# Two tiles' values weighed together in a Perceiver block's main loop, with a third place for the weights

## The chip, the cores and the metric

The kernel runs on one core of one Trainium2 chip. The metric is the device time of one execution in microseconds (us); the kernel before took 1071.89 us as the median of three runs (1071.27 to 1072.69). A core has five engines that run side by side, each with its own instruction stream: TensorE (PE in the profile; its weight loads are listed apart as PEld), VectorE (DVE), ScalarE (ACT), GpSimd (POOL) and SyncE (SP), which here only issues DMAs.

## The reference

One Perceiver layer on 128 queries of width 512: a cross attention to a context of 12544 rows, a self attention of the 128 queries, and a mixture of experts. The change lies in the cross attention alone (16 heads of width 32; the first 257 context rows are an image part with weights of their own, the other 12287 are the text part):

```python
q = rms_norm(linear(x, q_w, q_b), norm_q_w).reshape(B, L, NH, HD)
k = rms_norm(linear(ctx_txt, k_w, k_b), norm_k_w).reshape(B, -1, NH, HD)
v = linear(ctx_txt, v_w, v_b).reshape(B, -1, NH, HD)
...
img_x = attention(q, k_img, v_img)
txt_x = attention(q, k, v)
out = (txt_x + img_x).reshape(B, L, DIM)
return linear(out, o_w, o_b)
```

`attention` takes softmax of q·k / sqrt(32) over the context rows and weighs v with it. Each key row is divided by the root of its mean square, so the kernel needs a sum of squares for each context row. Everything is in fp32.

## The kernel before, in words

**Blocks and tiles.** The context comes transposed, in 25 blocks: block 0 is the image part (three tiles), blocks 1 to 24 are the text part, 512 rows each (511 in the last), in four tiles of 128 rows. The text tiles are numbered from t = 3; block 5 begins with tile 19, block 24 (`LAST`) with tile 95. In a block, j (0 to 3) is the tile's place. The main loop (line 1535) runs over the tiles of blocks 2 to 23. While it scores and weighs block b, it makes keys and values of block b + 1.

**Keys and values: seven products.** Instead of eight quarter products a block's keys (and likewise its values) come from seven, in the manner of Strassen and Winograd. `weight_sums` prepares sums of the weights once; `ctx_sums` (line 1058) prepares four sums of the context's quarters for each block on GpSimd: s1 and s2 for products 5 and 6, s4 and s3 for products 3 and 7. All four lie in one tile, `xsum`, with one buffer, so the sums for the next block wait until the last product of this one that reads them. `product` (line 1072) is one group of four matmuls in the program (eight in the trace, line 1082) and writes a PSUM bank from `bank()`, a ring of three that the sums of squares use too. Some products go on in the bank of an earlier one: 2 in that of 1, 3 in that of 5, 4 in that of 7. `step` (line 1131) issues product k for keys, values or both, and what empties the bank: ScalarE copies 1 and 2 (lines 1139, 1110, 1101), VectorE does the rest (1144, 1147, 1112, 1103). Once a half of the keys is complete (steps 3 and 4 for keys), ScalarE squares it (`squares`, line 1121), and `add_squares` (line 1123) adds the four chunks of 128 channels in two instructions on GpSimd.

**Norms.** `key_norms` (line 1010) lets TensorE add the squares over the channels, for two tiles at a time ([0, 1] or [2, 3]), VectorE scales the sums (line 1029), and GpSimd raises them to the power −1/2 into `rinv` (line 818).

**A tile.** `scores` (line 1159) is 16 matmuls on strips of 32 rows of the array into `ps_x`, the only score buffer (four PSUM banks). `weights` (line 1246) has VectorE multiply by `rinv`, subtract a per-query bound `m_bc` and write `p` (line 1255), and ScalarE take the exponential in place (line 1263). `weigh` (line 1266) is 16 matmuls on strips of 32 columns that add v weighted by p into one PSUM bank. `into_sums` (line 1424) adds p into the sum of weights on GpSimd (line 1433). The tiles `p` have two buffers in the pool `two`.

**The order.** Every instruction of the loop is kept in program order on its engine (`pin`), so the loop's text is the schedule of each engine. A tile's weights are weighed one tile later: iteration t computes its own scores, then weighs tile t − 1, and `into_sums` of tile t − 1 is issued ahead of that. Per j it goes:

- j = 0: product 1 of block b + 1; `into_sums`; `add_squares(b, 1)`; scores, `weigh`; product 2.
- j = 1: product 6; `into_sums`; scores, `weigh`, `key_norms(b, [2, 3])`.
- j = 2: product 5, product 7 for keys; `into_sums`, in six blocks (17 to 22, `AHEAD`) a scaling of weights on GpSimd; scores, `weigh`; product 3.
- j = 3: product 7 for values; `add_squares(b + 1, 0)`, `into_sums`, `ctx_sums(b + 2)` with all four sums; scores, `weigh`, `key_norms(b + 1, [0, 1])`; product 4; the load of block b + 3.

In block 23 products 7 and 4 of the last block are left to the code behind the loop (lines 1642 to 1676), which ends the attention: `step(b, 7, "k")`, norms, the weights of tile 95 (`p_last`, in the room of the value weights), the weighing of the tile left over, and so on.

**The room `mb`.** The tag `mb` in the pool `xc` first holds the bound from block 1's scores (`mb_txt`). From tile 13 on (`SWITCH`) the loop uses a later bound in another room. In block 15 the room gets codes of the self attention's third group of heads (`homes[2]`, lines 1633 to 1635), two loads of 512 KB; `early_loads` (line 1486) issues further such loads in the last block, as rooms come free.

```python
def weigh_pending():
    k, pk = pend
    weigh(k, pk, k in (t1, SWITCH), k == SWITCH - 1)
```

Of the kernel before, what the change touches and what calls it, by code (L numbers as in the profile page):

```python
# [9 lines left out]
FP = mybir.dt.float32  # L10
AF = mybir.ActivationFunctionType
ALU = mybir.AluOpType
# [758 lines left out]
def fast_block(ctx: ExitStack, tc: tile.TileContext, a: dict, out: bass.AP, amiss: bass.AP):  # L771
# [66 lines left out]
    def pin(ins):  # L838

        return tc.keep_in_program_order(ins)  # L840
# [55 lines left out]
    with ExitStack() as xs:  # L896
# [158 lines left out]

        left = {}

        def ctx_sums(b):

            q = quarters(ctx_sb[b])  # L1060
            t = xc.tile([P, 4, 2, HALF], FP, tag="xsum", name=f"xs_{b}")
            s1, s2, s3, s4 = (t[:, k, :, :] for k in range(4))
            sub = ALU.subtract
            pin(nc.gpsimd.tensor_tensor(s1, q[0, 1], q[1, 1], op=ALU.add))
            pin(nc.gpsimd.tensor_tensor(s2, s1, q[0, 0], op=sub))
            pin(nc.gpsimd.tensor_tensor(s4, q[1, 0], s2, op=sub))
            pin(nc.gpsimd.tensor_tensor(s3, q[0, 0], q[0, 1], op=sub))
            left[b] = {1: q[0, 0], 2: q[1, 0], 3: s4, 4: q[1, 1], 5: s1, 6: s2, 7: s3}

        vv, part_of, banks = {}, {}, {}  # L1070

# [414 lines left out]
        def early_loads(j):  # L1486

            if j == 0:
                f = slot(two, "kraw", "f")
                homes[2].append(f[0])  # L1490
                load_codes(2, "v", f[0])
                homes[3] = [f[1]]
                load_codes(3, "q", f[1])
                homes["bv"] = slot(two, "ctx", "bv")
                wo.append(slot(xc, "kw", "wo_0"))
            elif j == 1:
                g = slot(two, "v", "g")
                homes[3] += g
                load_codes(3, "k", g[0])
                load_codes(3, "v", g[1])  # L1500
                t = row("kt", "sc_23", (P, 2, 3 * GW))
                load_scales(2, t[:, 0, :])
                load_scales(3, t[:, 1, :])
                for k, of in enumerate((a["bv"][:1024], a["bv"][1024:])):
                    pin(nc.sync.dma_start(out=homes["bv"][k], in_=of.partition_broadcast(P)))
                wo.append(slot(two, "ctx", "wo_1"))
                wo.append(slot(xc, "xsum", "wo_2"))
                pin(nc.sync.dma_start(
                    out=so, in_=a["wo_scales"].unsqueeze(1).to_broadcast([FEAT // BLOCK, 2, D])
                ))  # L1510
                load_wo(0)
            elif j == 2:
                h = slot(xc, "sq", "h")
                homes[4] = list(h)
                load_codes(4, "q", h[0])
                load_codes(4, "k", h[1])
                t = row("vt", "sc_45", (P, 2, 3 * GW))
                load_scales(4, t[:, 0, :])
                load_scales(5, t[:, 1, :])
                pin(nc.sync.dma_start(out=bo, in_=a["bo"].partition_broadcast(P)))  # L1520
                wo.append(slot(xc, "vw", "wo_3"))
                load_wo(1)
                load_wo(2)
# [3 lines left out]
        def load_wo(k):  # L1527
            for h in range(2):
# [2 lines left out]
                    out=wo[k][h].rearrange("p (j f) -> p j f", j=2), in_=a["wo_codes"][:, j : j + 2, :]  # L1531
                ))

        AHEAD = range(NB - 8, NB - 2)
        for t in range(tile0[2], tile0[LAST]):
            b, part, o, m = tiles[t]
            j = t - tile0[b]


            make = step  # L1540
            if t == SWITCH + 3:
                pin(nc.tensor.matmul(
                    avp["txt"].rearrange("p g q -> p (g q)"),
                    lhsT=ident,
                    rhs=kept["av"],
                    start=False,
                    stop=False,
                    skip_group_check=True,
                ))
            late = make if b + 1 < LAST else (lambda *of: None)  # L1550
            if j == 0:
                make(b + 1, 1)
            elif j == 1:
                make(b + 1, 6)
            elif j == 2:
                make(b + 1, 5)
                late(b + 1, 7, "k")
            else:
                late(b + 1, 7, "v")
            if j == 3:  # L1560
                add_squares(b + 1, 0)
            if t == tile0[LAST] - 1:
                unsummed = pend
            else:
                into_sums(*pend)
            if j == 0:
                add_squares(b, 1)
            elif j == 2 and b in AHEAD:
                scale_weights((b - AHEAD[0]) // 3, "qkv"[(b - AHEAD[0]) % 3], nc.gpsimd)
            elif j == 3 and b + 2 < NB:  # L1570
                ctx_sums(b + 2)
            if t == SWITCH:
                m_bc["txt"] = m_new
            p, s = weights(t)
            weigh_pending()
            if j == 1:
                key_norms(b, [2, 3])
            elif j == 3 and b + 1 < LAST:
                key_norms(b + 1, [0, 1])
            pend = (t, p)  # L1580
            if t == tile0[RENEWED + 1]:
                m_new = xc.tile([P, 4, CHUNK], FP, tag="mx", name="mb_new")
                on_all(q_new, m_new, "new")
                pin(nc.vector.tensor_tensor(over, q_new, q_old, ALU.subtract))
                less = small.tile([P, XH], FP, tag="less", name="less")
                pin(nc.scalar.activation(less, over, AF.Exp, scale=-1.0))
            elif t == tile0[RENEWED + 1] + 1:

                shrink = rowp.tile([P, D], FP, tag="h", name="shrink")
                on_heads(less, shrink, "less")  # L1590
            elif t == SWITCH:
                av_old = avp["txt"].rearrange("p g q -> p (g q)")
                kept = {"av": row("kept_av", "kept_av")}
                pin(nc.vector.tensor_tensor(kept["av"], av_old, shrink, ALU.mult))
                avp["txt"] = ps_o.tile([P, NC, P], FP, tag="o", name="av_new")
            elif t == SWITCH + 2:
                lp = bank("l_old")
                for i in range(4):
                    r = slice(i * XHD, (i + 1) * XHD)
                    pin(nc.tensor.matmul(  # L1600
                        lp[r, :], lhsT=ones[:, :XHD], rhs=ls_old[i // 2][:, i % 2, :],
                        start=True, stop=True, skip_group_check=True,
                    ))
                kept["l"] = row("kept_l", "kept_l")
                pin(nc.vector.tensor_tensor(kept["l"], lp, shrink, ALU.mult))
            if j == 2:
                make(b + 1, 3, "k")
            if b <= RENEWED:
                largest(t, s)
            if j == 0:  # L1610
                make(b + 1, 2)
            elif j == 2:
                make(b + 1, 3, "v")
            elif j == 3:
                late(b + 1, 4)
                if b + 3 < NB:
                    load_ctx(b + 3)
            if t == tile0[RENEWED + 1] - 1:
                q_new = query_max(mx, P, "t1")
            if b == RENEWED + 3 and j == 0:  # L1620
                pin(nc.vector.reciprocal(l_img, l_img))
            if b == RENEWED + 3 and j == 1:
                flat = att_img.rearrange("p g q -> p (g q)")
                pin(nc.vector.tensor_tensor(flat, flat, l_img, ALU.mult))
            if b == RENEWED + 3 and j == 2:
                pin(nc.gpsimd.tensor_tensor(
                    att_img, att_img, vbs.unsqueeze(2).to_broadcast([P, NC, P]), op=ALU.add
                ))
            if b == AHEAD[0] - 2 and j == 0:
                for t_, nm in ((bq, "bq"), (bk, "bk"), (gw, "gate_w")):  # L1630
                    pin(nc.sync.dma_start(out=t_, in_=a[nm]))
                pin(nc.sync.dma_start(out=gb, in_=a["gate_bias"].partition_broadcast(P)))
                homes[2] = slot(xc, "mb", "q")
                load_codes(2, "q", homes[2][0])
                load_codes(2, "k", homes[2][1])
            if b == AHEAD[0] - 1 and j == 0:
                for g in range(2):
                    for nm, t in zip("qkv", homes[g]):
                        load_codes(g, nm, t)
                    load_scales(g, aw.tile([P, 3 * GW], FP, tag="sc", name=f"sc_{g}"))  # L1640
# [8 lines left out]
        key_norms(b, [0, 1])  # L1649
        ps = [weights(t, p=xc.tile([P, 4, CHUNK], FP, tag="vw", name="p_last"))[0]]  # L1650
        half_into_sums(unsummed[1], 1)
        weigh(k, p, False, False)
        half_into_sums(p, 0)
        step(b, 4, "k")
        add_squares(b, 1)
# [874 lines left out]
```

## Time and profile before

| what | value |
|---|---|
| median of the three runs | 1071.89 us (1071.27 to 1072.69) |
| the profiled execution: its own time | 1070.2 us |
| its span, from first to last instruction | 1068.5 us |
| TensorE clock granted | 0.998 of full speed |
| busy share of the span: PE, PEld, DVE, ACT, POOL | 98%, 77%, 51%, 33%, 65% |
| main loop from block 5's first scores to block 23's first scores (210.64 to 817.24) | 606.60 us, POOL busy 526.04, DVE 309.99, ACT 214.35 |
| from there to the VectorE work of `p_last` (844.18) | 26.94 us |
| DMA over the span | 106 GB/s mean, in the last 100 us about 400 |

A timeline row gives the start of a group of like instructions in us from the span's start, its length, the engine, the line, the operation, out<-in by the program's names, the shape and the count; a bracket at its end tells how long the engine was idle ahead of it and whose semaphore ended that. Ends of matmuls are modelled, so consecutive groups on PE overlap by some tenths of a microsecond: what a group costs is read from its start to the next one's start. In the chain the work that ended last is followed back from the end; its shares say which engine set the time.

### The profile page before, as it was taken

How to read it: one execution, taken by the hardware profiler on the slowest of the kernel's cores; microseconds unless marked ns; L12 is line 12 of the kernel's file. 1: busy time of each engine (PE TensorE's matmuls, PEld its weight loads, DVE VectorE, ACT ScalarE, POOL GpSimd, SP SyncE). 2: the span in 40 equal slices, each digit the busy share in tenths (PEclk: the TensorE clock that was granted, in tenths of full speed). 3: DMA queues.
4: the chain of work that ended last, by engine and by line, in shares of the span. 5: the costliest groups of instructions: out<-in, count | busy, mean ns of one | idle time of the engine just before them, and what ended most of it. 6: DMA issues, size and time to landing. Idle time of an engine off the chain costs nothing.

```text
span 1068.5 us, 24782 instructions
## 1 busy us (share of the span) xinstructions
PE 1051.4 (98%) x11076; PEld 826.6 (77%) x11076; DVE 541.1 (51%) x671; ACT 355.8 (33%) x438; POOL 694.8 (65%) x378
## 2 busy tenths in 40 slices
PE   9999999999999999999999999999999989999997
PEld 6778888888888888888888888888888769754332
DVE  3667854574445544455444554455444668432211
ACT  2353333333333333332333333333333424403111
POOL 2256888688988888888988789988899810000000
PEclk9999999999999999999999999999999999999999
DMA  8221021101111011110122301110110399619996
GB/s 318 86 81 41 2 87 44 41 1 41 40 41 40 2 40 41 40 36 7 41 84 106 99 26 41 41 40 3 39 41 2 123 361 382 229 64 410 415 413 247
DMA packets 43251, 113.24 MB, mean 106 GB/s; under 512 B 6720, under 2 KB 12032, under 8 KB 42112
## 3 DMA queue, kind: packets, MB, share of 16 engines
q1 hardware_dynamic: 43136, 111.57, 28.4%
q8 instruction: 89, 1.46, 0.5%
q14 instruction: 26, 0.21, 0.1%
HBM read 111.26 MB, written 0.29 MB: 104 GB/s over the span
## 4 chain that ended last, share of the span: by engine, by line
PE 92%; DVE 3%; POOL 2%; ACT 1%; DMA 1%; issue 0%; SPq 0%; DVEq 0%; ACTq 0%; POOLq 0%
PE kp L1082 28%; PE vp L1082 26%; PE sb L1166 9%; PE av_new L1272 8%; PE up L2117 5%; PE acc L2104 2%; PE qp L1776 1%; PE kp L1776 1%; PE yp L1934 1%; PE svp L1797 1%; PE y L2158 1%; PE vp L1234 1%; PE av_old L1272 1%; DVE p L1255 1%; DMA x<-in_x 1%; POOL sq L1127 1%
## 5 line engine op out<-in xcount | busy, mean ns | idle before, releaser
L1433 POOL TENSOR_TENSOR ls<-ls,p 128x2048 f32<-128x2048 f32 x79 | 359.7, 4553 | 21.3 <-ACT p L1263 21.3
L1263 ACT ACTIVATE p<-p 128x2048 f32<-128x2048 f32 (+1 forms) x95 | 179.9, 1894 | 444.5 <-DVE p L1255 432.9
L1255 DVE SCALAR_TENSOR_TENSOR p<-sb,rinv,mb_new 128x2048 f32<-128x2048 f32 (+1 forms) x86 | 200.0, 2326 | 129.4 <-POOL rinv L818 95.2
L1127 POOL TENSOR_TENSOR sq<-sq 128x512 f32<-128x512 f32 x96 | 96.0, 1000 | 98.2 <-ACT sq L1121 94.4
L1166 PEld LDWEIGHTS sb<-qT_txt,kraw 32*128 32x128 f32 (+1 forms) x3040 | 93.4, 186 | 32.0 <-issue 31.0
L1166 PE MATMUL sb<-qT_txt,kraw 32*128 32x128 f32 (+1 forms) x3040 | 111.5, 283 | 0.0
L1082 PE MATMUL kp<-xs,w_k_w 128*128 128x256 f32 x384 | 95.4, 391 | 0.0
L1082 PE MATMUL kp<-ctx,w_k_w 128*128 128x256 f32 x384 | 93.2, 386 | 1.0 <-ACT kp L1139 1.0
L1272 PE MATMUL av_new<-p,v 128*32 128x128 f32 (+1 forms) x2720 | 92.2, 276 | 1.0 <-ACT p L1263 1.0
L1082 PE MATMUL vp<-vt,xs 128*128 128x256 f32 x384 | 92.5, 384 | 0.0
L1082 PE MATMUL kp<-xs,kt 128*128 128x256 f32 x384 | 91.2, 380 | 0.1
L1082 PE MATMUL vp<-w_v_w,ctx 128*128 128x256 f32 x384 | 90.9, 380 | 0.0
L1082 PE MATMUL vp<-w_v_w,xs 128*128 128x256 f32 x384 | 90.8, 379 | 0.0
L1082 PEld LDWEIGHTS kp<-ctx,w_k_w 128*128 128x128 f32 x384 | 70.7, 190 | 15.0 <-issue 5.1
L1082 PEld LDWEIGHTS vp<-vt,xs 128*128 128x128 f32 x384 | 71.1, 190 | 13.3 <-ACT kraw L1110 4.5
L1082 PEld LDWEIGHTS kp<-xs,kt 128*128 128x128 f32 x384 | 72.5, 190 | 11.3 <-issue 1.1
L1082 PEld LDWEIGHTS vp<-w_v_w,xs 128*128 128x128 f32 x384 | 72.8, 190 | 10.1
L1082 PEld LDWEIGHTS vp<-w_v_w,ctx 128*128 128x128 f32 x384 | 72.8, 190 | 10.0 <-issue 0.2
L1272 PEld LDWEIGHTS av_new<-p,v 128*32 128x32 f32 (+1 forms) x2720 | 69.5, 109 | 12.3 <-ACT p L1263 2.1
L1082 PEld LDWEIGHTS kp<-xs,w_k_w 128*128 128x128 f32 x384 | 69.2, 189 | 12.6 <-issue 4.8
L818 POOL TENSOR_TENSOR rs_x<-ve_x,neghalf 128x1 f32<-128x1 f32 x3 | 1.7, 551 | 94.5 <-DVE ve_x L826 94.5
L1121 ACT ACTIVATE sq<-kraw 128x1024 f32<-128x1024 f32 x48 | 50.0, 1041 | 10.3 <-DVE kraw L1112 10.3
(460 smaller groups left out, 1442.3 us busy)
## 6 DMA issues: line engine op xcount, KB each, us to landing
ctx<-in_ctxT SPq DMA_DIRECT2D x23, 1024.0 KB, 4.9
wo<-in_experts SPq DMA_DIRECT2D x18, 512.0 KB, 9.0
wo<-in_wo_codes SPq DMA_DIRECT2D x8, 512.0 KB, 6.3
wq<-in_experts SPq DMA_DIRECT2D x8, 512.0 KB, 9.8
wk<-in_experts SPq DMA_DIRECT2D x8, 512.0 KB, 9.4
wv<-in_experts SPq DMA_DIRECT2D x7, 512.0 KB, 10.0
q<-in_experts SPq DMA_DIRECT2D x7, 512.0 KB, 10.1
f<-in_experts SPq DMA_DIRECT2D x7, 512.0 KB, 10.1
```

The source lines that it names most:

```text
L1082: pin(nc.tensor.matmul(t[:, h, :], lhsT=lhs, rhs=rhs, start=(first and h == 0 and c == 0), stop=(h == 1 and c == 1), skip_group_check=True,))
L1121: pin(nc.scalar.activation(sq[b][:, :, ks], kraw[b][:, :, ks], AF.Square))
L1127: pin(nc.gpsimd.tensor_tensor(sq[b][:, :w, ks], sq[b][:, :w, ks], sq[b][:, w : 2 * w, ks], op=ALU.add))
L1166: pin(nc.tensor.matmul(s[:m, i, g * P : (g + 1) * P], lhsT=kraw[b][rows, g, o : o + m], rhs=qT[part][rows, g, :], start=True, stop=True,))
L1234: pin(nc.tensor.matmul(vp[:m, :], lhsT=ctx_sb[0][:, c, o : o + m], rhs=vw["img"][:, c, :], start=(c == 0), stop=(c == NC - 1),))
L1255: pin(nc.vector.scalar_tensor_tensor(p[:m, k : k + n], s[:m, k : k + n], rinv[:m, t : t + 1], m_bc[part][:m, k : k + n], ALU.mult, ALU.sub ...
L1263: pin(nc.scalar.activation(p[:m, k : k + n], p[:m, k : k + n], AF.Exp))
L1272: pin(nc.tensor.matmul(avp[part][i * XHD : (i + 1) * XHD, g, :], lhsT=vv[b][:m, t - tile0[b], hd * XHD : (hd + 1) * XHD], rhs=p[:m, i, g * ...
L1433: pin(nc.gpsimd.tensor_tensor(d, d, src, op=ALU.add))
L1776: pin(nc.tensor.matmul(pp[:, k, :], lhsT=w[:, c, k * SHD : (k + 1) * SHD], rhs=hT2[:, c, :], start=(c == 0), stop=(c == NC - 1),))
L2104: pin(nc.tensor.matmul(acc, lhsT=lhsT, rhs=rhs, start=(n_acc == 0), stop=last))
L2117: pin(nc.tensor.matmul(up[r : r + m, :], lhsT=lhsT, rhs=w13_of((kind != "all", i), c), start=(c == 0), stop=(c == NC - 1), skip_group_chec ...
```

## The change

From block 5 (`PAIRED`) on, tiles are weighed in pairs: a tile with odd j is no longer weighed against by itself; at even j, behind the scores, both waiting tiles are weighed. For that a third place for weights is needed: each third tile's `p` lies in the room `mb`. The two loads of codes that used the room from block 15 on move to the head of `early_loads(0)` in the last block. The norms of tiles 2 and 3 move from j = 1 to j = 0, behind the pair. On GpSimd, `ctx_sums` is split: s1 and s2 stay where all four sums were; then, behind product 4, come `add_squares` of the second half (so far at j = 0 of the next block) and s4 and s3. In the code behind the loop both waiting tiles are weighed where one was.

```diff
-        def ctx_sums(b):
+        def ctx_sums(b, parts=(0, 1)):
 
             q = quarters(ctx_sb[b])
-            t = xc.tile([P, 4, 2, HALF], FP, tag="xsum", name=f"xs_{b}")
-            s1, s2, s3, s4 = (t[:, k, :, :] for k in range(4))
             sub = ALU.subtract
-            pin(nc.gpsimd.tensor_tensor(s1, q[0, 1], q[1, 1], op=ALU.add))
-            pin(nc.gpsimd.tensor_tensor(s2, s1, q[0, 0], op=sub))
-            pin(nc.gpsimd.tensor_tensor(s4, q[1, 0], s2, op=sub))
-            pin(nc.gpsimd.tensor_tensor(s3, q[0, 0], q[0, 1], op=sub))
-            left[b] = {1: q[0, 0], 2: q[1, 0], 3: s4, 4: q[1, 1], 5: s1, 6: s2, 7: s3}
+            if 0 in parts:
+                t = xc.tile([P, 4, 2, HALF], FP, tag="xsum", name=f"xs_{b}")
+                s1, s2, s3, s4 = (t[:, k, :, :] for k in range(4))
+                left[b] = {1: q[0, 0], 2: q[1, 0], 3: s4, 4: q[1, 1], 5: s1, 6: s2, 7: s3}
+                pin(nc.gpsimd.tensor_tensor(s1, q[0, 1], q[1, 1], op=ALU.add))
+                pin(nc.gpsimd.tensor_tensor(s2, s1, q[0, 0], op=sub))
+            if 1 in parts:
+                s2, s3, s4 = (left[b][k] for k in (6, 7, 3))
+                pin(nc.gpsimd.tensor_tensor(s4, q[1, 0], s2, op=sub))
+                pin(nc.gpsimd.tensor_tensor(s3, q[0, 0], q[0, 1], op=sub))
...
             if j == 0:
                 f = slot(two, "kraw", "f")
+                homes[2] = slot(xc, "mb", "q")
+                load_codes(2, "q", homes[2][0])
+                load_codes(2, "k", homes[2][1])
                 homes[2].append(f[0])
                 load_codes(2, "v", f[0])
...
+        PAIRED = RENEWED + 3
+        waiting = [pend]
...
-            if j == 0:
+            if j == 0 and b < PAIRED:
                 add_squares(b, 1)
             elif j == 2 and b in AHEAD:
                 scale_weights((b - AHEAD[0]) // 3, "qkv"[(b - AHEAD[0]) % 3], nc.gpsimd)
             elif j == 3 and b + 2 < NB:
-                ctx_sums(b + 2)
+                ctx_sums(b + 2, (0,) if b >= PAIRED - 1 else (0, 1))
             if t == SWITCH:
                 m_bc["txt"] = m_new
-            p, s = weights(t)
-            weigh_pending()
-            if j == 1:
+
+            p = None
+            if b >= PAIRED and (t - tile0[LAST]) % 3 == 0:
+                p = xc.tile([P, 4, CHUNK], FP, tag="mb", name=f"p_{t}")
+            p, s = weights(t, p=p)
+            if b < PAIRED or j % 2 == 0:
+                for k, pk in waiting:
+                    weigh(k, pk, k in (t1, SWITCH), k == SWITCH - 1)
+                waiting = []
+            waiting.append((t, p))
+            if j == (1 if b < PAIRED else 0):
                 key_norms(b, [2, 3])
             elif j == 3 and b + 1 < LAST:
                 key_norms(b + 1, [0, 1])
...
             elif j == 3:
                 late(b + 1, 4)
+                if b >= PAIRED - 1 and b + 1 < LAST:
+                    add_squares(b + 1, 1)
+                if b >= PAIRED - 1 and b + 2 < NB:
+                    ctx_sums(b + 2, (1,))
                 if b + 3 < NB:
                     load_ctx(b + 3)
...
-                homes[2] = slot(xc, "mb", "q")
-                load_codes(2, "q", homes[2][0])
-                load_codes(2, "k", homes[2][1])
...
-        weigh(k, p, False, False)
+        for k_, p_ in waiting:
+            weigh(k_, p_, False, False)
```

## The prediction

> **What bounds the kernel now.** I read the page's chain first, for the engine that sets the end.
>
> ```profile
> PE 92%; DVE 3%; POOL 2%; ACT 1%; DMA 1%; issue 0%; SPq 0%; DVEq 0%; ACTq 0%; POOLq 0%
> ```
>
> TensorE carries 92% of the chain, and in the main loop it never waits for data in the open; so the question is how its groups of matmuls follow one another. That is in the timeline, on PE alone. Call S a tile's scores (L1166), A the weighing of its values (L1272), Q the sums of squares turned into columns (L1018), P one of the seven block products for keys or values (L1082), and j the tile's place (0 to 3) in its block. Columns: start, length, group. Starts, not lengths, are to be read, since lengths overlap.
>
> ```profile
> 504.63 1.17 PE L1166 MATMUL sb<-qT_txt,kraw 32*128 32x128 f32 x32
> 505.74 1.08 PE L1272 MATMUL av_new<-p,v 128*32 128x128 f32 x32
> 506.63 0.28 PE L1018 MATMUL ssq<-ones,sq 128*32 128x1 f32 x16
> 506.85 1.99 PE L1082 MATMUL kp<-ctx,kt 128*128 128x256 f32 x8
> ...
> 513.95 1.17 PE L1166 MATMUL sb<-qT_txt,kraw 32*128 32x128 f32 x32
> 515.05 1.08 PE L1272 MATMUL av_new<-p,v 128*32 128x128 f32 x32
> 516.07 1.99 PE L1082 MATMUL kp<-ctx,w_k_w 128*128 128x256 f32 x8
> 517.89 1.89 PE L1082 MATMUL vp<-w_v_w,ctx 128*128 128x256 f32 x8
> 519.62 1.89 PE L1082 MATMUL kp<-xs,kt 128*128 128x256 f32 x8
> ```
>
> From start to start: S to A 1.10 us, A to P 1.02, A to Q 0.89, Q to P 0.22 (over many blocks 1.10, 1.01, 0.90 and 0.21), the first P after them 1.83, a later P 1.73, the last P before S 1.82 (512.13 to 513.95). A and Q have the same shape of the array (128*32); a change of shape costs about 0.1 us, staying in it does not. The scores start at 504.63, 513.95 and, further down the same view, 523.24, 530.83 and 538.32: a block takes 9.32 + 9.29 + 7.59 + 7.49 = 33.69 us.
>
> Three of these stretches equal the sum of their groups. The one from j = 0 to j = 1 doesn't: 1.10 + 1.02 + 1.83 + 2 × 1.73 + 1.82 = 9.22 against 9.30, so 0.08 us is a **stall**. The timelines of the other engines show it (in brackets the idle time ahead and who ended it):
>
> ```profile
> 503.80 2.07 POOL L1127 TENSOR_TENSOR sq<-sq 128x512 f32<-128x512 f32 x2 [3.95 <-ACT sq L1121]
> ...
> 515.51 0.70 POOL L818 TENSOR_TENSOR rinv<-ms,neghalf 128x2 f32<-128x2 f32 x1
> ...
> 516.24 2.35 DVE L1255 SCALAR_TENSOR_TENSOR p<-sb,rinv,mb_new 128x2048 f32<-128x2048 f32 x1 [4.95 <-POOL rinv L818]
> 518.62 1.91 ACT L1263 ACTIVATE p<-p 128x2048 f32<-128x2048 f32 x1 [3.98 <-DVE p L1255]
> 520.44 0.82 ACT L1110 ACTIVATE kraw<-kp,col_k_b 128x256 f32<-128x256 f32 x2
> 521.31 1.59 PEld L1082 LDWEIGHTS vp<-vt,xs 128*128 128x128 f32 x8 [0.20 <-ACT kraw L1110]
> ```
>
> The inverse norms `rinv` stand on GpSimd behind a sum of weights (4.55) and all four context sums (1.28 each); VectorE's `p` waits for them (it starts 2.3 us after its scores, at other j 1.31 to 1.34), so the exponential and behind it ScalarE's copy of product 2 are late, and product 6 has no PSUM bank.
>
> **The pairs.** Per block, A's were 2 × (A to P) + 2 × (A to Q) = 2 × 1.01 + 2 × 0.90 = 3.82 us. Now j = 0 has S A A Q P, j = 1 S P, j = 2 S A A P, j = 3 S Q P. A followed by A isn't in the trace. Its nearest row is A to Q, the same shape: 0.90; the other end is A to P, 1.01; the low end is the first to the last start in one A, 0.81. I take 0.90, as the last four of A's starts and the next four lie 0.1 apart within A already: 3 × 0.90 + 1.01 = 3.71, which is 0.11 less. S to P and S to Q, new in the loop, stand early in the trace:
>
> ```profile
> 52.95 1.17 PE L1166 MATMUL sa<-qT_txt,kraw 32*128 32x128 f32 x32
> 54.06 0.31 PE L1018 MATMUL ssq<-ones,sq 128*32 128x1 f32 x16
> 54.29 1.99 PE L1082 MATMUL vp<-vt,xs 128*128 128x256 f32 x8
> ...
> 76.76 1.17 PE L1166 MATMUL sb<-qT_txt,kraw 32*128 32x128 f32 x32
> 77.86 1.99 PE L1082 MATMUL kp<-xs,kt 128*128 128x256 f32 x8
> ```
>
> Both are 1.10, as S to A is. Q behind S takes 0.23, not 0.21. Net: 0.09 us a block.
>
> [...]
>
> **GpSimd's new order.** In j = 3: squares of the first half (2.07), a sum of weights (4.55), two context sums, `rinv`, squares of the second half, two more context sums, a sum of weights. `rinv` comes 2 × 1.28 = 2.6 us earlier than at 12.4 us behind the squares' start, so `p` of j = 0 no longer waits and the 0.08 stall goes. What is late next: product 6 for keys now takes the bank that product 2 holds, one P earlier than the values' product did, because Q's bank moved ahead of it. From scores to the end of the copy: 1.31 + 2.38 + 2.64 = 6.33 us (2.38 from `p` to the exponential and 2.64 from there to 521.26, both in the rows above). Its weight load, which runs 0.21 ahead of its matmul, is due 1.10 + 2 × 0.90 + 0.21 + 1.83 + 1.73 − 0.21 = 6.46 behind the scores. It fits by 0.1. Product 1 for keys waits for the bank that VectorE empties after product 4, which PE now starts 0.9 earlier behind its scores: 1.31 + 2.35 (`p`) + 0.07 + 0.88 (VectorE's two halves) + 0.05 = 4.66 against 1.10 + 0.23 + 1.83 + 1.73 − 0.21 = 4.68. If either is missed, a load late by 0.18 cost 0.08 here, and 0.10 (1.83 − 1.73) is what a product without early load costs: 0 to 0.10 each per block. I take 0, because both fit.
>
> The second half's squares must be there for Q at j = 0. Counted from the scores of j = 2: those of j = 3 start at 8.4, their exponential ends 5.6 later, ScalarE's square at 15.0. GpSimd begins the first half's squares at 3.01 + 2.04 + 0.88 + 1.04 + 0.08 = 7.05 and is free at 7.05 + 2.07 + 4.55 + 2.6 + 0.7 = 17.0, done with the second half at 19.0; Q stands at 8.39 + 8.44 + 1.10 + 2 × 0.90 = 19.7. The weights' sum behind it is 2.1 us later than now. With three places a place is wanted three tiles on; the tightest is that of j = 0, weighed 3 us behind the scores of j = 2 and wanted 6.7 us later. GpSimd's total stays: 28.4 us of 33.7, 31 with the scaling of weights.
>
> **Q right behind S at j = 3.** An A that stood between them is gone, and with it 0.9 us of cover. From the start of product 3 for keys PE now needs 1.83 + 1.73 + 1.82 + 1.10 = 6.48 us to Q; the sums need 2.04 (product and hand-over) + 0.88 (VectorE) + 1.04 (ScalarE) + 2.07 (GpSimd) + 0.15 = 6.2 (the 2.04 is VectorE's start behind such a product, 508.88 − 506.85; the exponential of j = 2, which now holds the square back by 0.6 us, is done by then, as product 3 starts 0.9 later behind its scores). Slack 0.3, before 0.7. Cost nothing, since the sums still come first.
>
> **The third place** is the room of the first bound, free in blocks 5 to 23 once the two loads are moved. The write to another buffer, `p_last`, takes the same 2.35, its sum 4.58. Cost nothing. **The two loads** (512 KB each) leave their old place at 547.01 and 547.48 and go to the head of the last block's early loads on SP, behind all context loads and ahead of the `f` loads at 839.44. Their place is free when the sum of tile 92 ends, some 2 us before that; two issues are 0.43 each. In the windows the DMA moves 0 GB/s from 836 to 840 and 260 from 840 to 844, later 170 to 250, so 1 MB fits; if that cover were gone, 1 MB at 410 GB/s is 2.6 us.
>
> **The tail.** From the scores of block 23's first tile to `p_last` on VectorE it takes 844.18 − 817.24 = 26.94 us. New: 10.22 (S A A Q P P P P) + 4.75 (S P P) + 3.01 (S A A) + 9.2 (product 3, squares 6.15, half a sum 2.37, `rinv` 0.7) = 27.18; and 0.90 less, as the first pair of block 5 holds one tile alone: 26.28. That is 0.66 less, and what follows hangs on `p_last`.
>
> **Sum.** 18 blocks (5 to 22) × (0.09 + 0.08) = 3.0, tail 0.7: **3.7 us less**. The profiled execution took 1070.2 us (span 1068.5): 1066.5. The median of the runs shown is 1071.89, 1.7 above it; on that scale, which is the one to be measured, 1068.2 (0.35% less). About 0.2%, 2.1 us, is what a measurement of this kernel can tell from no change; so faster begins below 1069.7.
>
> **Rivals.**
> 1. The bank waits stay or return: 0.10 for product 6, 0.10 for product 1. For it: margins of 0.13 and 0.02 us. Against: a late load is half hidden. One at its full price is 18 × 0.10 = 1.8 us: 1070.0; both, 1071.8; one at half its price is still faster. Chance 0.20, half of it within 0.2%. That the change doesn't do what it says, A after A costing 1.01 like any other change, ends beside it: 18 × 0.22 = 4.0, no gain, 1072; chance 0.05.
> 2. Slower: Q of j = 3 waits for GpSimd. It stands alone between two products, so a late sum stops TensorE in full. It decides when the chain of the squares is over 0.3 us longer; the saving is eaten at 0.3 + 3.7 / 19 = 0.5. One us longer costs 19 × 0.7 = 13 us: 1081. Against: the exponential ahead of the square ends 0.3 us before it is needed, and GpSimd is idle 3.95 us there (1.6 with scaling). Chance 0.10.
> 3. The two loads contend in the tail and cost their 2.6: 1070.8. For it: the DMA is full from 856 us on; against, they lie ahead of that. Chance 0.05.
>
> The forecast has 0.60.
>
> Range: 1066.5 (runs that lie as low as the profiled execution did) to 1071.8 (both bank waits); it leaves out the slower rival and little more. Faster 0.60 + 0.10 = 0.70; same 0.10 + 0.05 + 0.05 = 0.20; slower 0.10.
>
> **What would show it.** Right: scores 10.2, 6.5, 8.4 and 8.4 us apart, a block of 33.53; A to A 0.90; `p` at j = 0 starting 1.31 behind its scores; no PEld idle for ScalarE's `kraw`. Wrong: PE waiting at L1018 for `sq`, at L1082 for a bank, or a block that is not below 33.6.

## The result, and the profile after

| | before | after |
|---|---|---|
| median of six runs, us | 1071.76 (1071.27 to 1072.69) | 1067.1 (1066.76 to 1068.29) |
| ratio, with 95% interval | | 0.9963 [0.9953, 0.9973] |
| the profiled execution: time, span | 1070.2, 1068.5 | 1066.76, 1064.9 |
| from block 5's first scores to block 23's | 606.60 | 601.82 |
| from there to `p_last` on VectorE | 26.94 | 27.18 |
| from there to the span's end | 224.32 | 224.58 |
| ahead of block 5's first scores | 210.64 | 211.32 |
| scores to scores from j = 0 to 1, 1 to 2, 2 to 3, 3 to 0 (medians) | 9.30, 7.59, 7.49, 9.32 | 10.19, 6.48, 8.37, 8.44 |
| a block: their sum | 33.70 | 33.48 |

The change makes the kernel faster by 0.37% (0.27 to 0.47%), some 4 us; the medians lie 4.7 apart. It comes out of the main loop, 4.78 us there: 18 × 0.22 = 4.0, and 0.87 for one weighing that now falls behind block 23's first scores. The other three stretches give back 0.24, 0.26 and 0.68. The last of these is no effect of the change: the kernel's first scores already start 0.67 later (53.62 for 52.95), far ahead of the first changed instruction, and block 5 began between 210.64 and 212.10 in the nine profiles of this study. The 0.26 is no larger than the spread of that stretch either, 224.3 to 224.9 in all profiles but that of experiment 4.

TensorE is still the bound. First the chain's shares, then the timeline of PE over one block of the kernel after, in the columns used before:

```profile
PE 94%; DVE 3%; ACT 1%; DMA 1%; POOL 1%; issue 0%; SPq 0%; DVEq 0%; ACTq 0%; POOLq 0%
```

```profile
511.76 1.17 PE L1169 MATMUL sb<-qT_txt,kraw 32*128 32x128 f32 x32
512.86 1.95 PE L1275 MATMUL av_new<-p,v 128*32 128x128 f32 x64
514.63 0.28 PE L1018 MATMUL ssq<-ones,sq 128*32 128x1 f32 x16
...
529.53 1.96 PE L1275 MATMUL av_new<-p,v 128*32 128x128 f32 x64
531.42 1.99 PE L1085 MATMUL kp<-xs,w_k_w 128*128 128x256 f32 x8
```

A pair is one row of 64 matmuls. From its start to Q it takes 1.77 us (512.86 to 514.63), to a product 1.89 (529.53 to 531.42). The starts of the single matmuls divide the pair: the second tile's first matmul starts at 513.76, so A to A is 0.90, as A to Q was; from there it is 0.87 to Q, and in the other pair 0.99 to the product, where an A right behind scores takes 0.90 and 1.01. The 0.02 lies at the very start of an A: behind scores its second four matmuls start 0.13 after the first four and each later four 0.11 after those ahead, in the second A of a pair all of them 0.11. There is no idle time in brackets: nothing in the block waits in the open.

The waits of VectorE for GpSimd's inverse norms show the other half of the change. First the line of before, then that of after (total us, times, longest):

```profile
DVE p L1255 <- POOL rinv L818: 95.2, 20, 5.0
```

```profile
DVE p L1258 <- POOL rinv L818: 0.6, 1, 0.6
```

The wait that came once in each block is gone. What followed from it is seen in the timeline of the other engines after:

```profile
511.88 2.09 POOL L1130 TENSOR_TENSOR sq<-sq 128x512 f32<-128x512 f32 x2
...
513.10 2.35 DVE L1258 SCALAR_TENSOR_TENSOR p<-sb,rinv,mb_new 128x2048 f32<-128x2048 f32 x1 [4.00 <-PE sb L1169]
...
517.30 0.82 ACT L1113 ACTIVATE kraw<-kp,col_k_b 128x256 f32<-128x256 f32 x2
...
518.19 1.70 PEld L1085 LDWEIGHTS kp<-xs,kt 128*128 128x128 f32 x8
```

`p` of j = 0 starts 1.34 us behind its scores (511.76) and waits for those scores alone; ScalarE's copy ends at 518.12, and product 6 for keys loads its weights at 518.19 without idle time.

### The profile page after: what moved, and what is told of

The parts are those of the page before. It is cut to its first block, busy times and chain, and to the rows that moved or that the text cites. A ratio compares the mean times of both kernels' runs of the same rounds, so it can differ in the third digit from the quotient of the medians.

```text
span 1064.9 us, 24839 instructions
## 1 busy us (share of the span) xinstructions
PE 1047.9 (98%) x11076; PEld 829.6 (78%) x11076; DVE 538.2 (51%) x671; ACT 360.1 (34%) x438; POOL 694.2 (65%) x378
## 4 chain that ended last, share of the span: by engine, by line
PE 94%; DVE 3%; ACT 1%; DMA 1%; POOL 1%; issue 0%; SPq 0%; DVEq 0%; ACTq 0%; POOLq 0%
PE kp L1085 28%; PE vp L1085 27%; PE sb L1169 10%; PE av_new L1275 7%; PE up L2135 5%; PE acc L2122 2%; PE qp L1794 1%; PE kp L1794 1%; PE yp L1952 1%; PE svp L1815 1%; PE y L2176 1%; PE vp L1237 1%; PE av_old L1275 1%; PE ssq L1018 1%; DVE p L1258 1%; DMA x<-in_x 1%
## 5 line engine op out<-in xcount | busy, mean ns | idle before, releaser
L1275 PE MATMUL av_new<-p,v 128*32 128x128 f32 (+1 forms) x2720 | 84.6, 274 | 0.5 <-ACT p L1266 0.5
L1275 PEld LDWEIGHTS av_new<-p,v 128*32 128x32 f32 (+1 forms) x2720 | 71.8, 110 | 7.1 <-ACT p L1266 1.4
L1147 DVE TENSOR_TENSOR kz<-kp,kp 128x512 f32<-128x512 f32 x24 | 16.6, 691 | 98.5 <-issue 93.9
```

The source lines that it names most:

```text
L1147: pin(nc.vector.tensor_tensor(piece(kind, "z"), t, part_of[kind, "p1"], ALU.add))
L1275: pin(nc.tensor.matmul(avp[part][i * XHD : (i + 1) * XHD, g, :], lhsT=vv[b][:m, t - tile0[b], hd * XHD : (hd + 1) * XHD], rhs=p[:m, i, g * ...
```

## The experiments

All intervals below are medians over the blocks 5 to 22. A ratio is to the runs of the kernel before on the same chip (medians 1071.76 for the change, 1071.42 for experiments 1 to 4, 1071.5 for 5 to 7). Experiments 4 and 5 have a single time and no interval.

| kernel | time, us | ratio to before, 95% | j0→1, 1→2, 2→3, 3→0 | block |
|---|---|---|---|---|
| before | 1071.76 | | 9.30, 7.59, 7.49, 9.32 | 33.70 |
| the change | 1067.1 | 0.9963 [0.9953, 0.9973] | 10.19, 6.48, 8.37, 8.44 | 33.48 |
| 1. GpSimd's order alone | 1070.08 | 0.9987 [0.9979, 0.9996] | 9.22, 7.59, 7.49, 9.32 | 33.62 |
| 2. pairs, GpSimd's old order | 1070.14 | 0.9982 [0.9974, 0.9991] | 10.09, 6.72, 8.37, 8.44 | 33.62 |
| 3. the two loads alone | 1071.41 | 0.9994 [0.9986, 1.0003] | 9.30, 7.59, 7.49, 9.32 | 33.70 |
| 4. the change, GpSimd's old order | 1234.29 | | 18.65, 6.48, 8.37, 8.44 | 41.94 |
| 5. the change, longer squares | 1077.19 | | 10.19, 6.48, 8.37, 8.92 | 33.96 |
| 6. pairs at odd j | 1067.59 | 0.9965 [0.9951, 0.9978] | 8.34, 8.46, 6.48, 10.19 | 33.47 |
| 7. pairs at odd j, copy first | 1065.73 | 0.9945 [0.9931, 0.9958] | 8.21, 8.46, 6.48, 10.19 | 33.34 |

My theory was that the gain has two parts, a stall that goes (0.08 a block) and one change of the array's shape fewer (12 to 11 a block, 0.11). Its rivals: all of it comes from GpSimd; the pairs gain by themselves, whatever stands behind them; the slack of the squares is not what the trace says. Where nothing else is said, diffs are against the kernel with the change.

**1. GpSimd's order alone.** No pairs, no third place, loads at their old place:

```diff
...
-            p, s = weights(t, p=p)
-            if b < PAIRED or j % 2 == 0:
-                for k, pk in waiting:
-                    weigh(k, pk, k in (t1, SWITCH), k == SWITCH - 1)
-                waiting = []
-            waiting.append((t, p))
-            if j == (1 if b < PAIRED else 0):
+            p, s = weights(t)
+            for k, pk in waiting:
+                weigh(k, pk, k in (t1, SWITCH), k == SWITCH - 1)
+            waiting = [(t, p)]
+            if j == 1:
                 key_norms(b, [2, 3])
...
```

> GpSimd's new order alone: the context sums in two parts with the second half's squares between them; one tile weighed at a time, two places, norms of tiles 2 and 3 at j = 1 and the two loads where they were before. Theory (the ledger of the prediction): only the stall goes, 0.08 us a block; scores of j = 0 and j = 1 are 9.22 apart in place of 9.30, a block takes 33.62, 1.4 us less in all. Rival 1, the order alone makes the whole gain: 33.48 a block, 3.9 us less. Rival 2, it makes nothing: 33.70.

Only the interval from j = 0 to j = 1 moves, 9.30 to 9.22, which is the sum of its groups. So the stall was 0.08, and it hung on GpSimd's order. The rest of the gain, more than half, is not there.

**2. The pairs with GpSimd's old order**, Q of the second half back at j = 1:

```diff
-            if j == 0 and b < PAIRED:
+            if j == 0:
                 add_squares(b, 1)
...
-                ctx_sums(b + 2, (0,) if b >= PAIRED - 1 else (0, 1))
+                ctx_sums(b + 2)
...
-            if j == (1 if b < PAIRED else 0):
+            if j == 1:
                 key_norms(b, [2, 3])
...
-                if b >= PAIRED - 1 and b + 1 < LAST:
-                    add_squares(b + 1, 1)
-                if b >= PAIRED - 1 and b + 2 < NB:
-                    ctx_sums(b + 2, (1,))
```

> Pairs, third place and moved loads, but GpSimd's order as before, and so the norms of tiles 2 and 3 stay at j = 1, apart from the pair. Theory: weighing in pairs pays only where the norms stand behind a pair, as each change of the array's shape costs 0.11 and there are twelve again: A's 2 x (0.87 + 1.01) = 3.77 for 3.82, Q behind S 0.02 dearer twice, nothing net; the 0.08 of the stall goes for another reason, the second A at j = 0 covers it, although p at j = 0 still starts over 2 us late. A block 33.62, with the tail 2.1 us less in all. Rival 1, the pairs as such make the gain: 33.5. Rival 2, the stall stays because the inverse norms stay late: 33.70.

This settles what a pair is worth. Here Q at j = 1 stands between scores and a product, so the block still has 12 changes of shape, and the pairs save none. The block is 33.62, as in experiment 1, and for another reason. The timelines of VectorE and PE:

```profile
516.56 2.35 DVE L1258 SCALAR_TENSOR_TENSOR p<-sb,rinv,mb_new 128x2048 f32<-128x2048 f32 x1 [5.45 <-POOL rinv L818]
```

```profile
513.77 1.17 PE L1169 MATMUL sb<-qT_txt,kraw 32*128 32x128 f32 x32
...
522.04 1.89 PE L1085 MATMUL vp<-vt,xs 128*128 128x256 f32 x8
523.86 1.17 PE L1169 MATMUL sb<-qT_txt,kraw 32*128 32x128 f32 x32
```

`p` still waits for `rinv`, 2.79 us behind its scores, but the second A puts PE 0.87 later at product 6, which covers it: product 6 takes its usual 1.82. GpSimd's order and the pair each remove the same stall, so their gains do not add. The pair brings its own part only where Q stands right behind it.

**3. The two loads alone**, in the kernel before:

```diff
             if j == 0:
                 f = slot(two, "kraw", "f")
+                homes[2] = slot(xc, "mb", "q")
+                load_codes(2, "q", homes[2][0])
+                load_codes(2, "k", homes[2][1])
...
-                homes[2] = slot(xc, "mb", "q")
-                load_codes(2, "q", homes[2][0])
-                load_codes(2, "k", homes[2][1])
```

> The kernel before, with only the two loads of 512 KB moved to the head of the last block's early loads. Theory: no difference (within 0.3 us), as the DMA is idle there. Rival: they push the loads behind them, up to 2.6 us more.

The interval of the ratio takes in no change, and from block 5's first scores on every stretch is that of before within 0.1 us (606.59, 26.93 and 224.36). Moving 1 MB into the tail costs nothing that can be measured.

**4. The change with GpSimd's old order**, Q at j = 0 left behind the pair: experiment 2 without its edit to `key_norms`.

```diff
-            if j == 0 and b < PAIRED:
+            if j == 0:
                 add_squares(b, 1)
...
-                ctx_sums(b + 2, (0,) if b >= PAIRED - 1 else (0, 1))
+                ctx_sums(b + 2)
...
-                if b >= PAIRED - 1 and b + 1 < LAST:
-                    add_squares(b + 1, 1)
-                if b >= PAIRED - 1 and b + 2 < NB:
-                    ctx_sums(b + 2, (1,))
```

> The whole change but for GpSimd's order, which is as before: the norms of tiles 2 and 3 stand behind the pair at j = 0, while the second half's squares are added only behind all four context sums and a sum of weights. Theory: TensorE waits at Q of j = 0, which is due 19.7 us behind the scores of j = 2 while the squares end at 26.1: about 6.4 us a block, 115 us in all, about 1182. Rival: GpSimd catches up because it has idle time, a wait below 2 us a block, below 1105.

The wait came as expected; the price was 8.46 a block, not 6.4, and the time 1234.29, not about 1182. The timeline of PE and the windows (busy time of PE, PEld, DVE, ACT, POOL, then the granted clock, the DMA's share and GB/s) show why:

```profile
634.39 1.96 PE L1275 MATMUL av_new<-p,v 128*32 128x128 f32 x64
642.62 0.40 PE L1018 MATMUL ssq<-ones,sq 128*32 128x1 f32 x16 [6.27 <-POOL sq L1130]
642.95 3.78 PE L1085 MATMUL kp<-ctx,w_k_w 128*128 128x256 f32 x8
646.52 2.04 PE L1085 MATMUL vp<-w_v_w,ctx 128*128 128x256 f32 x8
648.39 1.89 PE L1085 MATMUL kp<-xs,kt 128*128 128x256 f32 x8
```

```profile
640.00:643.00 3.00, 0.38 (x17) 0.37 (x17) 0.00 (x0) 0.38 (x1) 2.49 (x3) 0.50 0.00 0
643.00:647.00 4.00, 4.00 (x13) 3.25 (x11) 0.16 (x1) 0.24 (x1) 3.68 (x2) 0.52 0.02 4
647.00:652.00 5.00, 5.00 (x28) 4.13 (x26) 0.69 (x1) 1.19 (x3) 1.51 (x1) 1.00 0.00 0
```

From the pair to Q it is 8.23 instead of 1.77, the wait's own 6.46. From 640 us on, some 3.7 into the wait, the granted clock is at half (from 638 to 640 it was 1.00), and it stays there until shortly before 647. So Q takes 0.33 (instead of 0.22), the product behind it 3.57 (instead of 1.83), the next one 1.87 (instead of 1.73): 6.46 + 0.11 + 1.74 + 0.14 = 8.45. My expectation had counted the wait alone. What the time has beyond 18 × 8.46 lies in the tail, where `p_last` comes 9.4 us later than in the change, and in single longer waits. Full clock comes again some 4.2 us after PE's restart at 642.62, an estimate from the mean of 0.59 between 646 and 647; from 647 on it is 1.00.

**5. The slack at j = 3.** One more GpSimd instruction between the first half's squares and Q, a multiplication by one that changes no value:

```diff
                 add_squares(b + 1, 0)
+                if b >= PAIRED - 1:
+                    first = sq[b + 1][:, :1, :HALF]
+                    pin(nc.gpsimd.tensor_tensor(first, first, ones[:, 0:1].unsqueeze(1).to_broadcast([P, 1, HALF]), op=ALU.mult))
```

> The changed kernel with one more instruction on GpSimd between the first half's squares and the weights' sum at j = 3 (the squares' sums multiplied by 1, some 0.73 us, 0.80 with the hand-over). Theory (the slower rival of the prediction): Q right behind the scores has 0.27 us of slack and no cover behind it, so TensorE waits 0.8 - 0.27 = 0.53 us in each of 18 blocks, 9.5 us more than the changed kernel, about 1076.5. Rival: the wait is hidden by loads of weights ahead or by GpSimd's idle time, below 2 us more.

Only the interval from j = 3 to j = 0 moves, by 0.48. GpSimd and PE in that block, and the wait over the whole run:

```profile
507.12 2.07 POOL L1130 TENSOR_TENSOR sq<-sq 128x512 f32<-128x512 f32 x2 [3.26 <-ACT sq L1124]
509.27 0.61 POOL L1572 TENSOR_TENSOR sq<-sq,ones 128x256 f32<-128x256 f32 x1
```

```profile
508.37 1.17 PE L1169 MATMUL sb<-qT_txt,kraw 32*128 32x128 f32 x32
509.94 0.30 PE L1018 MATMUL ssq<-ones,sq 128*32 128x1 f32 x16 [0.40 <-POOL sq L1572]
```

```profile
PE ssq L1018 <- POOL sq L1572: 7.8, 19, 0.7
```

The squares end at 509.19 and the added instruction at 509.88, 0.69 later; Q starts 1.57 behind its scores instead of 1.10. So 0.69 more work costs 0.47, and 0.22 of it was hidden. The trace of the change gives 0.27 for the same place (squares end at 504.15, Q starts at 504.42), of which the hand-over takes 0.06 (509.88 to 509.94 here). The wait comes 19 times; the main stretch is 9.25 us longer than the change's, the tail 0.69, and the time 10 us above its median, 5.7 above that of the kernel before on the same chip (1071.5). The slower rival's mechanism is real, and only 0.2 to 0.3 us away.

**6. Pairs at odd j.** If a change of shape is what counts, both Q's should stand behind a pair: ten changes a block.

```diff
-            if b < PAIRED or j % 2 == 0:
+            if b < PAIRED or j % 2 == 1:
                 for k, pk in waiting:
...
-            if j == (1 if b < PAIRED else 0):
+            if j == 1:
                 key_norms(b, [2, 3])
```

> The changed kernel with the pairs weighed at odd j in place of even j, so that both groups of norms (j = 1 and j = 3) stand behind a pair and no pair is followed by a product. Theory: ten changes of the array's shape a block where there were eleven: 0.14 less, 33.34, but the values' product 6 at j = 0 loses the cover of the pair and waits for the bank of product 2, 0.1, and product 7 for values at j = 2 nearly 0.05: 33.45 to 33.48, as the changed kernel. Rival: the banks are free in time, 33.34 and 2.5 us less than the changed kernel. Other rival: the pair at odd j waits for the exponential of the tile just before it, 33.7 or more.

The block stays at 33.47. The weight loads say where the gain went:

```profile
519.50 1.59 PEld L1085 LDWEIGHTS vp<-vt,xs 128*128 128x128 f32 x8 [0.27 <-ACT kraw L1113]
```

Without a pair behind its scores, j = 0 reaches product 6 for values too early: its bank waits for ScalarE's copy, and from its start to the next scores it takes 1.93 instead of 1.82 (8.34 for the interval, 8.21 the sum of its groups). The 0.14 that the better place of Q saves went into that bank.

**7. The same, with the copy ahead of the exponential.** On ScalarE the copy of product 2 for keys stands behind the exponential of `p`, though its data are there first (in experiment 6 the product's row on PE, a modelled end, runs to 516.19, the exponential starts at 516.82 and the copy at 518.63). Against experiment 6:

```diff
+        def exp_of(t, p):
+            m = tiles[t][3]
+            pin(nc.scalar.activation(p[:m], p[:m], AF.Exp))
+
-        def weights(t, s=None, p=None, parts=1):
+        def weights(t, s=None, p=None, parts=1, exp=True):
...
-                pin(nc.scalar.activation(p[:m, k : k + n], p[:m, k : k + n], AF.Exp))
+                if exp:
+                    pin(nc.scalar.activation(p[:m, k : k + n], p[:m, k : k + n], AF.Exp))
...
-            p, s = weights(t, p=p)
+            p, s = weights(t, p=p, exp=b < PAIRED or j != 0)
...
-                make(b + 1, 2)
+                make(b + 1, 2, "k")
+                if b >= PAIRED:
+                    exp_of(t, p)
+                make(b + 1, 2, "v")
```

> As the one with pairs at odd j, and ScalarE empties product 2 of the keys ahead of the exponential at j = 0. Theory: the bank is free 2.4 us earlier, so the wait at product 6 goes: 33.36 a block, 2.2 us less than the changed kernel, 6 us less than before: 1065 to 1066. Rival: the exponential, 0.2 us later, makes something else late, as much as with the other order or more.

ScalarE and PE:

```profile
515.42 0.84 ACT L1113 ACTIVATE kraw<-kp,col_k_b 128x256 f32<-128x256 f32 x2 [2.44 <-PE kp L1085]
516.15 1.91 ACT L1251 ACTIVATE p<-p 128x2048 f32<-128x2048 f32 x1
```

```profile
518.67 1.89 PE L1085 MATMUL vp<-vt,xs 128*128 128x256 f32 x8
520.49 1.17 PE L1169 MATMUL sb<-qT_txt,kraw 32*128 32x128 f32 x32
```

The copy ends at 516.26, 2.2 us before the weights of product 6 for values are loaded (518.46), and the product takes its 1.82 again. The block is 33.34 and the median 1065.73 (five runs, 1065.44 to 1066.13), faster than before by 0.42 to 0.69% and below each run of the change (1066.76 to 1068.29), though these were not taken side by side. Experiment 6, taken beside it, had 1067.08 to 1069.4.

## Why the prediction was right

The forecast was 1068.2 and the median is 1067.1, faster as forecast. Step by step:

- **The order of the groups.** All four intervals came within 0.04 us of the forecast, S to Q and S to P at 1.10 as the early rows had them.
- **A to A.** It is 0.90, as forecast. The term that was mis-sized stands right behind it: the forecast gave the second A of a pair the same 0.90 to Q and 1.01 to a product as an A behind scores, and it takes 0.87 and 0.99. Twice a block that is 0.05, and it is the whole difference between the forecast block (33.53) and the measured one (33.48), 0.9 us over 18 blocks.
- **One change of shape fewer.** Experiments 2, 6 and 7 bear it out: no gain with twelve changes, 0.14 with eleven (0.22 less the stall's 0.08), 0.14 more with ten once the bank is free. The rows' 0.11 holds, but it is only what the way out costs (A to P for A to Q, 1.01 for 0.90). The way in costs 0.02 besides: an A or a Q right behind scores takes 0.02 longer than one behind an A. The forecast counted this 0.02 where Q lost its A (j = 3), and not where the second A's gained theirs (j = 0 and j = 2), so it had 0.09 for 0.14.
- **The stall.** 0.08 a block, gone (experiment 1). But the forecast gave all of it to GpSimd's order; experiment 2 shows that the pair alone would have covered it too.
- **The margins.** Product 6 for keys fits by 0.07 (forecast 0.13). Product 1 for keys fits by 0.17 (forecast 0.02): VectorE's two halves end at 507.83, the load is at 508.00. The second half's squares end 0.66 ahead of Q (forecast 0.7), the first half's 0.27 ahead (forecast 0.3; 0.22 by experiment 5).
- **The third place and the loads** cost nothing, as forecast; experiment 3 tested the loads by themselves. The third place was not tried alone, but in experiment 2, which has it, each interval is the sum of its groups.
- **The tail** took 27.18, the forecast figure, and 0.87 less in the stretch ahead of it for the single tile of the first pair. The step behind it did not hold: the forecast let the rest hang on `p_last`, and in the chain of before it does, but in that of after the time from the scores at 838.44 to those at 849.42 is TensorE's own, and `p_last` is not on it. It cost little: the next-to-last tile's weighing starts 14.72 us behind `p_last` (855.04), before 14.64 (858.82).
- **The scale.** The forecast for the profiled execution was 1066.5 and it took 1066.76. The 1.7 us from there to the median were added because before's profile lay that far below its runs; after's lies 0.3 below. That offset did not come again, and it is why the median came out 1.1 below the forecast while the profiled time was 0.3 above. Even the 0.3 is in part luck: the loop and the tail gave 4.5 (4.78 less 0.24) where 3.7 was forecast, and 0.9 went into the two stretches (0.26 and 0.68) that the forecast took to stay as they were.

Of the rivals, the bank wait did not come here but did in experiment 6, at 0.11 where 0.10 was its price. The slower one, a Q that waits for GpSimd, did not come; experiment 5 shows that it is decided where the prediction put it, and experiment 4 that a long wait of this kind costs more than the time by which GpSimd is late (8.46 us a block for a wait of 6.46).

## What to carry to other kernels

On an engine that is never idle, list the start-to-start time of each group and count the changes of shape; moving a short piece of work behind a neighbour of its own shape saved 0.14 us each time here, while grouping work whose neighbours stay different saved nothing (33.62 in experiment 2, as in experiment 1 without the pairs). Each such move takes cover from a chain that runs beside it: work out that chain's slack first (0.27, 0.66, 0.17 and 0.07 us here), and look on the engines beside it for a bulk instruction that stands ahead of the one that is waited for, as the context sums (1.28 us each) stood ahead of `rinv` and the exponential (1.91 us) ahead of the copy. Where two edits can each remove the same stall, try each alone before their gains are added.

## What the runs showed of the hardware that I had not expected

- A wait of TensorE in each block cost more than its length: 6.46 us of wait, then 1.99 us more for work at half the granted clock (experiment 4). The 19 waits of 0.4 us in experiment 5 left the mean clock of its run at 0.999.
- A late weight load cost less than its lateness. The load of a product behind another product ran 0.21 us ahead of its matmuls (519.41 for 519.62, before); late by 0.18 it cost 0.08 (before), and late by all of it, 0.23 (519.50 for 519.27), it cost 0.11 and the 0.02 by which the matmuls themselves began late (experiment 6). On the line through these two (0.08 and 0.13 in all) a lateness of 0.1 would cost nothing, an estimate; no run here had one.
